# Softmax normalization moved from the output stage to each tile's exit from PSUM, and key tiles reused for value-output weights, in a latent-attention block

## The chip, the cores and the metric

The kernel runs on one core of one Trainium2 chip. A core has four compute engines that run side by side, each with its own instruction queue: TensorE (PE in the profile; its weight loads are listed as PEld), VectorE (DVE), ScalarE (ACT) and GpSimd (POOL). SyncE (SP) only issues transfers. Engines wait for each other through semaphores, and within one queue the instructions run in order: one that waits holds all behind it. POOL's queue, like SP's, can issue DMAs too; such an issue occupies POOL for a time. The metric is the device time of one execution in microseconds (us). The runs shown of the kernel before took 1716.29 us in the median of three (1714.57 to 1717.13).

## The reference

One transformer block on 2048 tokens of width 512, in fp32: attention with low-rank queries and keys/values (16 heads, query rank 384, latent rank 128, head size 128 plus 64 of rotary position), residual and layer norm, then a linear layer with residual and layer norm.

```python
cq   = rms_norm(x @ w_qa.T, q_a_ln_w);  q = (cq @ w_qb.T)        # 16 heads of 128 + 64
ckv  = x @ w_kva.T                                               # 128 + 64
k_pe = rope(ckv[..., 128:]);            ckv_l = rms_norm(ckv[..., :128], kv_a_ln_w)
kv   = ckv_l @ w_kvb.T;                 k_nope, v = split(kv)    # per head
scores = where(causal, -inf, concat(q_nope, rope(q_pe)) @ concat(k_nope, k_pe).T * scale)
attn = softmax(scores)
x = layernorm(x + (attn @ v) @ w_o.T)
x = layernorm(x + x @ (weight * scale[:, None]).T + bias)
```

The softmax's division is what the change is about: every row of `attn @ v` has to be divided by the sum of that row's exponentials at some point.

## The kernel before

**What is kept.** The key half of `w_kvb` is folded into the queries, so that keys are the latent itself. `Kn` (latent, 128 rows) and `Kp` (position) lie in SBUF for all 2048 tokens, each as two fp32r parts whose sum is the fp32 value (`[P, 2, S]`, 16 KB in each partition). `V` is the same latent with tokens on the partitions, as two f16 parts. The value half of `w_kvb` is folded into `w_o`: for each pair of heads a tile `wvo` (`[P, 2, 2, HID]` fp32r, 8 KB in each partition) takes the latent result straight to the output. There are eight pairs of heads.

**Attention.** Queries come in four blocks b = 0 to 3 of 512, each in four tiles qt of 128. For each block, pair p, tile qt and head j, `head_scores` makes the scores by TensorE (L437, mask L440), takes the row maximum on VectorE (L500), and exponentiates on ScalarE (L522), whose accumulator gives the row sums. `head_probs` cuts the probabilities in two f16 parts (ScalarE L553, POOL L554). `turn` transposes them, by VectorE in squares of 32 (L536) and by a DMA on SP's queue through a place in SBUF called `ring`. `values` (L593) multiplies by V on TensorE (L604), in two halves, and lets the result leave PSUM by a ScalarE copy (L609) into a tile `ot`, 128 latent rows by 256 columns (two heads of 128 queries). `put_off` stores `ot` to `ot_d[b][p]` in DRAM: on POOL's queue in block 0 (L321), later on SP's (L329). In block 0 the two heads go together (`pair_scores`, `pair_probs`, L561 to L591), since a tile has at most 512 keys.

**Sums.** `sums_of` gives one small tile for each block and pair, with a column for each tile and head. `settle` runs once a pair is complete: it adds the two halves where a row of scores is cut in two (b > 1, L462), takes the reciprocal of 128 x 8 (L463, L465), transposes it (L467) so that the reciprocals lie along rows, and stores them to `inv_d[b][p]` on SP's queue (L468). All 512 x 2 of a pair go into one such store.

**Output stage.** For each block it takes the pairs in turn. `latent_load` loads the pair's 512 KB of `ot_d` (`o`, L800), and `inv_d` broadcast over the partitions (`iv`, another 512 KB, L806). `latent_split` multiplies the one by the other on POOL (L818) and cuts the product in two fp32r parts, `oh` on ScalarE (L64) and `ol` on VectorE (L65). `accumulate` multiplies by `wvo` on TensorE (L856), 24 matmuls for a pair of a block. Then residual and layer norm (L936 to L952, with POOL at L944), the linear layer (L977) and the second layer norm. The output stage of block 0 and the making of `wvo` (`value_output`, L197, cut at L67 and L68) begin among the last values of block 3.

**Order and memory.** Block 0 is ordered by the scheduler throughout. From block 1 on, TensorE and SP keep the program's order, and VectorE and ScalarE too in the last part of attention; VectorE, ScalarE and POOL otherwise get the order that the scheduler found. Pool `blk` has two buffers for each tag, `ot` among them. The PSUM pool `m`, which values use, has four buffers in block 0 and two later. `wvo0` and `wvo1` lie in the pool `pcr`, `wvo2` and `wvo3` in a pool `pcq` (L895), `wvo4` to `wvo6` in `pc`, which opens where Kn, Kp and V are given up (L918), and `wvo7` in `pcr`.

Of the kernel before, what the change touches and what calls it, by code (L numbers as in the profile page):

```python
# [9 lines left out]
F16 = mybir.dt.float16  # L10
BF16 = mybir.dt.bfloat16
F32 = mybir.dt.float32
F32R = mybir.dt.float32r
# [36 lines left out]
def mla_block(ctx: ExitStack, tc: tile.TileContext, a, out):  # L50
# [22 lines left out]
    wpe_d = [dram.tile([P, 2, LT, 256], F32R, name=f"wpe_d{g}") for g in range(4)]  # L73
    ot_d = [[dram.tile([P, 4, 256], F32, name=f"ot_d{b}_{p}") for p in range(NPAIR)] for b in range(NB)]

    inv_d = [[dram.tile([4, 32, 32], F32, name=f"inv_d{b}_{p}") for p in range(NPAIR)] for b in range(NB)]


    ident = const.tile([P, P], F32, name="ident")
# [21 lines left out]
    ctx_kv = ctx.enter_context(ExitStack())  # L101

    ctx.enter_context(tc.tile_pool(name="pad_l", bufs=1)).tile([P, 8], F32, name="pad_l")
    kv = ctx_kv.enter_context(tc.tile_pool(name="kv", bufs=1))
    Kn = kv.tile([P, 2, S], F32R, name="Kn")
    Kp = kv.tile([P, 2, S], F32R, name="Kp")
    V = [kv.tile([P, 2, 4, P], F16, name=f"V{b}") for b in range(NB)]

# [336 lines left out]
                return mask  # L445
            mask()

    def sums_of(b, p):

        if ("sums", b, p) not in state:  # L450
            state["sums", b, p] = small.tile([P, 2 if b > 1 else 1, 8], F32, tag="sums", name=f"sums{b}_{p}", bufs=2)
            due.append((b, p))
        return state["sums", b, p]

    def settle(now=None):

        while due and due[0] != now:
            b, p = due.pop(0)
            sums = state.pop(("sums", b, p))
            pad = state["pads"][p % 2]  # L460
            if b > 1:
                nc.vector.tensor_tensor(pad[:, :8], sums[:, 0], sums[:, 1], ALU.add)  # L462
                nc.vector.reciprocal(pad[:, :8], pad[:, :8])  # L463
            else:
                nc.vector.reciprocal(pad[:, :8], sums[:, 0])  # L465
            inv = small.tile([P, 32], F32, tag="inv", name=f"inv{b}_{p}", bufs=2)
            nc.vector.transpose(inv, pad)  # L467
            nc.sync.dma_start(inv_d[b][p].rearrange("g t q -> (g t) q"), inv)  # L468

# [3 lines left out]
    def head_scores(pools, b, p, j, qt, nk, prev):  # L473
# [40 lines left out]
        for ti, (v, c0, n, w) in enumerate(tiles):  # L514

            if ti == 0 or b == 3:
                size = nk if b == 2 else n * w
                pr = pools[1].tile([P, size], F32, tag="pr", name=f"pr{b}_{p}_{qt}_{j}_{ti}", bufs=(5, 4, 5)[b - 1])
                parts.append((pr, c0, []))
            x = c0 - parts[-1][1]  # L520
            parts[-1][2].append(slice(x, x + n * w))
            nc.scalar.activation(  # L522
                pr[:, x : x + n * w].rearrange("p (a c) -> p a c", a=n),
                v,
                AF.Exp,
                bias=bias,
                scale=r,
                accum_out=sums_of(b, p)[:, ti, 2 * qt + j : 2 * qt + j + 1],
            )
        return parts  # L530

# [29 lines left out]
    def pair_scores(pool, b, p, qt, nk):  # L561
# [11 lines left out]
        for j in range(2):  # L573
            nc.scalar.activation(  # L574
                pr[:, j, :],
                ps[:, j, :nk],
                AF.Exp,
                bias=bias[:, j : j + 1],
                scale=r,
                accum_out=sums_of(b, p)[:, 0, 2 * qt + j : 2 * qt + j + 1],  # L580
            )
        return pr

# [9 lines left out]
    def values(b, p, qt, nk, PT):  # L593

        kts = nk // P
        v = (PT() if b else PT)[:, : 4 * nk].rearrange("p (q j k r a) -> p j a k q r", j=2, q=4, a=2, k=kts)
        ps = psum["m"].tile([P, 512], F32, tag="m", name=f"o{b}_{p}_{qt}")
        n = 0
        for k in range(kts):
            if k == kts // 2:  # L600
                yield
            vt = V[k // 4]
            for i, l in ((0, 0), (0, 1), (1, 0)):
                nc.tensor.matmul(  # L604
                    ps[:, :256], vt[:, i, k % 4, :], v[:, :, l, k, :], start=n == 0, stop=n == 3 * kts - 1
                )
                n += 1
        ot = blk.tile([P, 256], F32, tag="ot", name=f"ot{b}_{p}_{qt}")
        nc.scalar.activation(ot, ps[:, :256], AF.Copy)  # L609
        put_off(ot_d[b][p][:, qt, :], ot)  # L610
        yield

# [66 lines left out]
    def units(pool, ring, b):  # L679
        lag = min(ring.shape[1] // (2048 * (b + 1)) - 1, 3) if b else 2  # L680

        for p in range(NPAIR):
# [24 lines left out]
            for qt in range(4):  # L707
# [7 lines left out]
                else:  # L715
                    s0, PT = None, place(ring, 2048 * (b + 1), 4 * nk, (b, p) == (2, NPAIR - 1) and qt > 0)
                if nk <= 512:
                    pi = pair_scores(pool, b, p, qt, nk)
                    flush()
                    probs.append(pair_probs(pool, b, p, qt, nk, PT, pi))  # L720
                    if qt == 1:
                        settle((b, p))
                    fill()
                    next(side[0], None)
                    if p and qt % 2:
# [4 lines left out]
                    run_values(lag)  # L730
                else:
                    for j in range(2):
                        if 2 * qt + j == 1:
                            settle((b, p))
                        prepare_output(b, p, 2 * qt + j)
                        prev = probs.pop() if probs else iter(())
                        pi = head_scores(pool, b, p, j, qt, nk, prev)
# [58 lines left out]
    ohl = []  # L796

    def latent_load(b, p, by=nc.sync.dma_start):
        o = state["pcr"].tile([P, 4, 256], F32, tag="o", name=f"o{b}_{p}")
        by(o, ot_d[b][p])  # L800

        n, pool, tag = (4, state["pcr"], "iv") if b == 0 and p < 4 else (1, blk, "qn")
        iv = [pool.tile([P, 4, 8 // n, 32], F32, tag=tag, name=f"iv{b}_{p}_{i}", bufs=2) for i in range(n)]
        for i, v in enumerate(iv):
            src = inv_d[b][p][:, 8 // n * i : 8 // n * (i + 1)].rearrange("g t q -> g (t q)")
            by(v.rearrange("p g t q -> p g (t q)"), src.partition_broadcast(P))  # L806
        state["o", b, p] = o, iv

    def latent_split(b, p):
        if b == NB - 1 and p >= 4:  # L810
            oh, ol = ohl[p - 4]
        else:
            oh = state["pcr"].tile([P, 4, 256], F32R, tag="oh", name=f"oh{b}_{p}")
            ol = state["pcr"].tile([P, 4, 256], F32R, tag="ol", name=f"ol{b}_{p}")
        o, iv = state.pop(("o", b, p))
        parts = o.rearrange("p t q -> p (t q)").rearrange("p (n t g q) -> p n t g q", n=len(iv), g=4, q=32)
        for i, v in enumerate(iv):
            nc.gpsimd.tensor_tensor(parts[:, i], parts[:, i], v.rearrange("p g t q -> p t g q"), ALU.mult)  # L818
        split(o, oh, ol)
        return oh, ol  # L820

    def latent(b, p):
# [58 lines left out]
    with tc.manual_schedule(engines={ET.PE, ET.SP}), ExitStack() as ctx_f:  # L881
# [10 lines left out]

        ps_a = ctx.enter_context(tc.tile_pool(name="ps_a", bufs=4, space=PSUM, reuse_waits="tile"))
        accs = [ps_a.tile([P, HID], F32, tag="acc", name=f"acc0_{t}") for t in range(4)]
        pcq = ctx.enter_context(tc.tile_pool(name="pcq", bufs=1, side="right", reuse_waits="tile"))  # L895
        wvo = state["wvo"]
        wvo += [pcq.tile([P, 2, 2, HID], F32R, name=f"wvo{EARLY + i}") for i in range(2)]
        load_wo(2, blk, "pe")
        latent_load(0, EARLY + 1)
        load_wo(3, blk, "qn")  # L900
# [194 lines left out]
```

## Time and profile before

| | |
|---|---|
| median of the runs shown | 1716.29 us (1714.57 to 1717.13) |
| profiled execution, its own time | 1721.02 us |
| span of the profiled execution | 1719.2 us |
| mean granted TensorE clock | 0.967 |
| attention, query block 0 | about 76 to 265 us |
| block 1; block 2; block 3 | about 265 to 530; 530 to 890; 890 to 1384 us |
| output stage | about 1384 to 1719 us |

The page counts an engine as busy while an instruction of its runs; a DMA-issuing instruction is not counted, though its queue is held by it. Rows of the groups read: line, engine, operation, written tile <- read tiles, shape, count | busy time in all and mean ns of one | idle time just before them and what ended it. A row of a DMA reads: written <- read, issuing engine, count, size of each, median time from issue to landing. For those that the change touches:

```profile
iv<-inv_d SPq DMA_DIRECT2D x28, 512.0 KB, 6.0
```

16 more broadcast loads of `iv` have 128 KB each (block 0, pairs 0 to 3, four for each pair). By shape, the eviction of values at L609 takes 352, 382 and 411 ns (least, median, most), from 76.0 to 1429.9 us.

### The profile page before, as it was taken

What the parts mean: (1) busy time and instruction counts of PE and PEld (TensorE: products, weight loads), DVE (VectorE), ACT (ScalarE), POOL (GpSimd) and SP (SyncE); (2) the same over time, 40 slices, a digit from 0 to 9 for tenths busy, and PEclk for the clock granted to TensorE, in tenths of its full rate; (3) what the DMA queues carried; (4) which work ended last, traced back from release to release, by engine and by line L of the source; (5) the groups of instructions that cost most, each with busy time, mean ns of one, the idle gap of its engine ahead of it and who ended that gap; (6) DMA issues with size and microseconds to landing.
All of it is one profiled execution on the core that took longest, in us unless ns stands there. A gap on an engine that the chain in (4) does not pass through costs nothing. (4 is left out here: it accounts for less than half of the span.)

```text
span 1719.2 us, 27373 instructions
## 1 busy us (share of the span) xinstructions
PE 1597.6 (93%) x9292; PEld 1309.0 (76%) x9292; DVE 1109.0 (65%) x1650; ACT 936.3 (54%) x1593; POOL 836.9 (49%) x606
## 2 busy tenths in 40 slices
PE   8898997999999999999999999999999758888878
PEld 7787876888888888888878888787887536667656
DVE  6567665667677777777766786777677524534364
ACT  5556565566667767677656666566666423111120
POOL 2355663455545655565555556555556432423241
PEclk9899998999999999999999999999999879999989
DMA  7879675667676676666766667557666555445340
GB/s 217 259 211 284 171 213 160 152 184 197 168 222 189 182 178 173 162 174 158 216 169 173 153 156 181 150 133 180 155 165 168 153 158 192 157 123 169 129 137 35
DMA packets 272939, 296.79 MB, mean 173 GB/s; under 512 B 44161, under 2 KB 243201, under 8 KB 271777
## 3 DMA queue, kind: packets, MB, share of 16 engines
q1 hardware_dynamic: 261216, 267.62, 57.8%
q0 software_dynamic: 4672, 17.73, 3.5%
q10 hardware_dynamic: 6912, 9.70, 1.8%
q8 instruction: 74, 1.21, 0.3%
q14 instruction: 65, 0.52, 0.1%
HBM read 99.94 MB, written 35.65 MB: 79 GB/s over the span
## 5 line engine op out<-in xcount | busy, mean ns | idle before, releaser
L554 POOL TENSOR_TENSOR hlpr<-pr,hlpr 128x1024 f16<-128x1024 f32 (+3 forms) x320 | 613.8, 1938 | 499.6 <-ACT hlpr L553 466.0
L437 PE MATMUL s<-Kn,qn 128*128 128x512 f32 (+4 forms) x1920 | 511.8, 374 | 13.8 <-ACT pr L574 8.2
L522 ACT ACTIVATE pr<-s,bias,rq 128x1024 f32<-128x1024 f32 (+3 forms) x320 | 325.3, 1021 | 317.3 <-issue 194.3
L500 DVE TENSOR_REDUCE neg<-s 128x1 f32<-128x1024 f32 (+3 forms) x320 | 311.1, 986 | 157.8 <-PE s L440 90.7
L604 PE MATMUL o<-ring,V 128*128 128x256 f16 x3024 | 376.2, 275 | 9.3 <-DMA ring<-pr 5.5
L437 PEld LDWEIGHTS s<-Kn,qn 128*128 128x128 f32 x1920 | 335.8, 189 | 62.7 <-ACT pr L574 9.3
L536 DVE STREAM_TRANSPOSE pr<-hlpr 128x1024 f32<-128x1024 f32 (+7 forms) x256 | 311.2, 1223 | 97.1 <-POOL hlpr L554 71.8
L437 PE MATMUL s<-Kp,pe 128*128 128x512 f32 (+4 forms) x1280 | 363.6, 364 | 8.2 <-DMA pe<-prod 7.3
L604 PEld LDWEIGHTS <-V 128*128 128x128 f16 x3264 | 302.9, 97 | 86.1 <-issue 34.4
L553 ACT ACTIVATE hlpr<-pr 128x1024 f16<-128x1024 f32 (+3 forms) x320 | 337.8, 1114 | 3.9
L437 PEld LDWEIGHTS s<-Kp,pe 128*128 128x128 f32 x1280 | 234.4, 190 | 39.7 <-DMA pe<-prod 7.5
L818 POOL TENSOR_TENSOR o<-o,iv 128x1024 f32<-128x1024 f32 (+1 forms) x44 | 80.1, 1825 | 191.6 <-DMA o<-ot_d 107.9
L856 PE MATMUL acc<-wvo,oh 128*128 128x512 f32 x448 | 151.1, 419 | 3.4 <-ACT oh L64 2.1
L409 PE MATMUL ps_qn<-cq,wq 128*128 128x512 f32 x576 | 149.4, 405 | 5.0 <-DMA wq<-wq_d 4.7
L409 PEld LDWEIGHTS ps_qn<-cq,wq 128*128 128x128 f32 x576 | 105.8, 192 | 25.4 <-DVE pr L536 3.4
L856 PE MATMUL acc<-wvo,ol 128*128 128x512 f32 x224 | 94.4, 421 | 24.4 <-DVE ol L65 24.4
L856 PEld LDWEIGHTS acc<-wvo,oh 128*128 128x128 f32 x448 | 88.7, 201 | 26.2 <-issue 4.3
L64 ACT ACTIVATE oh<-o 128x1024 fp32r<-128x1024 f32 x28 | 29.6, 1058 | 106.7 <-POOL o L818 88.3
L609 ACT ACTIVATE ot<-o 128x256 f32<-128x256 f32 x128 | 48.5, 379 | 63.5 <-PE o L604 54.0
L68 DVE SCALAR_TENSOR_TENSOR qn<-ps_qn,kvln,qn 128x512 fp32r<-128x512 f32 x64 | 47.5, 743 | 50.3 <-ACT qn L67 50.1
L589 POOL TENSOR_TENSOR hl<-pr,hl 128x128 f16<-128x128 f32 (+3 forms) x64 | 56.8, 907 | 44.4 <-ACT hl L588 44.1
L856 PEld LDWEIGHTS acc<-wvo,ol 128*128 128x128 f32 x224 | 44.9, 200 | 38.6 <-DVE ol L65 28.6
(154 smaller groups left out, 1568.1 us busy)
## 6 DMA issues: line engine op xcount, KB each, us to landing
ring<-pr SPq DMA_DIRECT2D x384, 128.0 KB, 2.7
wq<-wq_d SPq DMA_DIRECT2D x22, 768.0 KB, 5.7
o<-ot_d SPq DMA_DIRECT2D x32, 512.0 KB, 5.9
ring<-pr SPq DMA_DIRECT2D x128, 112.0 KB, 2.6
iv<-inv_d SPq DMA_DIRECT2D x28, 512.0 KB, 6.0
ot_d<-ot SPq DMA_DIRECT2D x97, 128.0 KB, 2.6
ring<-pr SPq DMA_DIRECT2D x128, 96.0 KB, 2.4
ring<-pr SPq DMA_DIRECT2D x64, 192.0 KB, 3.5
```

Source lines behind the costliest of these rows:

```text
L409: nc.tensor.matmul(ps, w[:, i, lt, j * P : (j + 1) * P], cq[:, k, lt, :], start=n == 0, stop=n == 8)
L437: nc.tensor.matmul(ps[:, :w], lhs, K[:, i, c0 : c0 + w], start=n == 0, stop=n == 4 and not by_product)
L500: nc.vector.tensor_reduce(neg[:, ti : ti + 1], v, axis=AX.XY, op=ALU.max, negate=True)
L522: nc.scalar.activation(pr[:, x : x + n * w].rearrange("p (a c) -> p a c", a=n), v, AF.Exp, bias=bias, scale=r, accum_out=sums_of(b, p)[:, ...
L536: nc.vector.transpose(sq.rearrange("p (k c r) -> p k c r", k=4, r=32), words.rearrange("p (c k r) -> p k c r", k=4, r=32))
L553: nc.scalar.activation(hl[:, 0, c], pr[:, c], AF.Copy)
L554: nc.gpsimd.tensor_tensor(hl[:, 1, c], pr[:, c], hl[:, 0, c], ALU.subtract)
L589: nc.gpsimd.tensor_tensor(hl[:, j, 1, :], pr[:, j, :], hl[:, j, 0, :], ALU.subtract)
L604: nc.tensor.matmul(ps[:, :256], vt[:, i, k % 4, :], v[:, :, l, k, :], start=n == 0, stop=n == 3 * kts - 1)
L609: nc.scalar.activation(ot, ps[:, :256], AF.Copy)
L818: nc.gpsimd.tensor_tensor(parts[:, i], parts[:, i], v.rearrange("p g t q -> p t g q"), ALU.mult)
L856: nc.tensor.matmul(acc, l[:, t, c], state["wvo"][p][:, i, j, :], start=p == 0 and j == 0 and n == 0, stop=p == NPAIR - 1 and j == 1 and n ...
```

## The change

Four things are done.

- The sums get one tile for each block, pair and tile of queries (three buffers), and `settle` runs at the start of every tile: a reduction over the two halves where there are two, a reciprocal of 128 x 2, a transpose, and a store of 16 KB into a rotating DRAM tile `rows` (eight buffers). The store is issued from POOL's queue, where it was SP's.
- `values` allocates a tile `iv` of 128 x 256 under the tag `ot`, which has two buffers in all, and loads `rows` into it, broadcast over the partitions: 128 KB in pieces of 256 bytes, from POOL's queue. The result leaves PSUM by a VectorE multiply with `iv`, in place of the ScalarE copy. There are 128 such tiles, so 128 stores, 128 loads and 128 multiplies.
- In the output stage the `iv` loads and the POOL multiplies go; `latent_split` only splits. In all POOL's queue goes from 544 to 746 instructions, SP's from 736 to 667, ScalarE's from 1181 to 1054 and VectorE's from 1597 to 1967.
- V moves into a pool of its own, and the pool of Kn and Kp lives to the end. `wvo2` to `wvo5` are written into the two halves of Kn and of Kp; pool `pcq` is gone, and `pc` holds `wvo6` alone.

```diff
-    inv_d = [[dram.tile([4, 32, 32], F32, name=f"inv_d{b}_{p}") for p in range(NPAIR)] for b in range(NB)]
...
-    kv = ctx_kv.enter_context(tc.tile_pool(name="kv", bufs=1))
+    kv = ctx.enter_context(tc.tile_pool(name="kv", bufs=1))
+    vals_ = ctx_kv.enter_context(tc.tile_pool(name="vals", bufs=1))
...
-    V = [kv.tile([P, 2, 4, P], F16, name=f"V{b}") for b in range(NB)]
+    V = [vals_.tile([P, 2, 4, P], F16, name=f"V{b}") for b in range(NB)]
...
+    def sums_of(b, p, qt):
+
+        key = b, p, qt
+        if ("sums", *key) not in state:
+            state["sums", *key] = small.tile([P, 2, 2 if b > 1 else 1], F32, tag="sums", name=f"sums{b}_{p}_{qt}", bufs=3)
+            due.append(key)
+        return state["sums", *key]
+
+    def settle(now=None, last=None):
+
+        while due and due[0] != now and (last is None or last in due):
+            key = due.pop(0)
+            sums = state.pop(("sums", *key))
+            pad = state["pads"][key[2] % 2]
+            if key[0] > 1:
+                nc.vector.tensor_reduce(pad[:, :2], sums, axis=AX.X, op=ALU.add)
+                nc.vector.reciprocal(pad[:, :2], pad[:, :2])
             else:
-                nc.vector.reciprocal(pad[:, :8], sums[:, 0])
-            inv = small.tile([P, 32], F32, tag="inv", name=f"inv{b}_{p}", bufs=2)
+                nc.vector.reciprocal(pad[:, :2], sums[:, :, 0])
+            name = "_".join(map(str, key))
+            inv = small.tile([P, 32], F32, tag="inv", name=f"inv{name}", bufs=2)
             nc.vector.transpose(inv, pad)
-            nc.sync.dma_start(inv_d[b][p].rearrange("g t q -> (g t) q"), inv)
+            rows = state["rows", *key] = dram.tile([4, 32, 32], F32, tag="rows", name=f"rows{name}", bufs=8)
+            nc.gpsimd.dma_start(rows.rearrange("g t q -> (g t) q"), inv)
...
         ps = psum["m"].tile([P, 512], F32, tag="m", name=f"o{b}_{p}_{qt}")
+        settle(last=(b, p, qt))
+        iv = blk.tile([P, 256], F32, tag="ot", name=f"iv{b}_{p}_{qt}")
+        rows = state.pop(("rows", b, p, qt))[:, :2].rearrange("g t q -> g (t q)")
+        nc.gpsimd.dma_start(iv.rearrange("p (g x) -> p g x", g=4), rows.partition_broadcast(P))
...
         ot = blk.tile([P, 256], F32, tag="ot", name=f"ot{b}_{p}_{qt}")
-        nc.scalar.activation(ot, ps[:, :256], AF.Copy)
+        views = [x.rearrange("p (j g q) -> p j g q", j=2, g=4) for x in (ot, ps[:, :256])]
+        nc.vector.tensor_tensor(*views, iv.rearrange("p (g j q) -> p j g q", g=4, j=2), ALU.mult)
         put_off(ot_d[b][p][:, qt, :], ot)
...
                 if nk <= 512:
+                    settle()
                     pi = pair_scores(pool, b, p, qt, nk)
                     flush()
                     probs.append(pair_probs(pool, b, p, qt, nk, PT, pi))
-                    if qt == 1:
-                        settle((b, p))
...
-                        if 2 * qt + j == 1:
-                            settle((b, p))
+                        if j == 0:
+                            settle()
...
     def latent_load(b, p, by=nc.sync.dma_start):
-        o = state["pcr"].tile([P, 4, 256], F32, tag="o", name=f"o{b}_{p}")
+        o = state["o", b, p] = state["pcr"].tile([P, 4, 256], F32, tag="o", name=f"o{b}_{p}")
         by(o, ot_d[b][p])
-
-        n, pool, tag = (4, state["pcr"], "iv") if b == 0 and p < 4 else (1, blk, "qn")
-        iv = [pool.tile([P, 4, 8 // n, 32], F32, tag=tag, name=f"iv{b}_{p}_{i}", bufs=2) for i in range(n)]
-        for i, v in enumerate(iv):
-            src = inv_d[b][p][:, 8 // n * i : 8 // n * (i + 1)].rearrange("g t q -> g (t q)")
-            by(v.rearrange("p g t q -> p g (t q)"), src.partition_broadcast(P))
-        state["o", b, p] = o, iv
...
-        o, iv = state.pop(("o", b, p))
-        parts = o.rearrange("p t q -> p (t q)").rearrange("p (n t g q) -> p n t g q", n=len(iv), g=4, q=32)
-        for i, v in enumerate(iv):
-            nc.gpsimd.tensor_tensor(parts[:, i], parts[:, i], v.rearrange("p g t q -> p t g q"), ALU.mult)
-        split(o, oh, ol)
+        split(state.pop(("o", b, p)), oh, ol)
...
-        pcq = ctx.enter_context(tc.tile_pool(name="pcq", bufs=1, side="right", reuse_waits="tile"))
         wvo = state["wvo"]
-        wvo += [pcq.tile([P, 2, 2, HID], F32R, name=f"wvo{EARLY + i}") for i in range(2)]
+        wvo += [K[:, i].rearrange("p (a j h) -> p a j h", a=2, j=2) for K in (Kn, Kp) for i in range(2)]
...
-    wvo += [pc.tile([P, 2, 2, HID], F32R, name=f"wvo{p}") for p in range(EARLY + 2, NPAIR - 1)]
+    wvo += [pc.tile([P, 2, 2, HID], F32R, name=f"wvo{p}") for p in range(EARLY + 4, NPAIR - 1)]
```

More of the change, by code (lines that the diff above doesn't have):

```diff
@@ L446, in score @@
             mask()
[L448 to L463, printed above, removed]
-            else:
-                nc.vector.reciprocal(pad[:, :8], sums[:, 0])
-            inv = small.tile([P, 32], F32, tag="inv", name=f"inv{b}_{p}", bufs=2)
+    def sums_of(b, p, qt):
[12 more added lines that the diff above has]
+                nc.vector.reciprocal(pad[:, :2], pad[:, :2])
+            else:
+                nc.vector.reciprocal(pad[:, :2], sums[:, :, 0])
+            name = "_".join(map(str, key))
+            inv = small.tile([P, 32], F32, tag="inv", name=f"inv{name}", bufs=2)
             nc.vector.transpose(inv, pad)
-            nc.sync.dma_start(inv_d[b][p].rearrange("g t q -> (g t) q"), inv)
+            rows = state["rows", *key] = dram.tile([4, 32, 32], F32, tag="rows", name=f"rows{name}", bufs=8)
+            nc.gpsimd.dma_start(rows.rearrange("g t q -> (g t) q"), inv)
     def head_scores(pools, b, p, j, qt, nk, prev):
@@ L527, in head_scores @@
                 scale=r,
-                accum_out=sums_of(b, p)[:, ti, 2 * qt + j : 2 * qt + j + 1],
+                accum_out=sums_of(b, p, qt)[:, j, ti : ti + 1],
             )
@@ L579, in pair_scores @@
                 scale=r,
-                accum_out=sums_of(b, p)[:, 0, 2 * qt + j : 2 * qt + j + 1],
+                accum_out=sums_of(b, p, qt)[:, j, 0:1],
             )
```

## The prediction

> **What bounds the kernel now.** I read the page's totals and its 40 slices first, then busy time by stretch, cut where the stages change, then the waits and the order of time around the gaps. Totals and slices:
>
> ```profile
> PE 1597.6 (93%) x9292; PEld 1309.0 (76%) x9292; DVE 1109.0 (65%) x1650; ACT 936.3 (54%) x1593; POOL 836.9 (49%) x606
> ...
> PE   8898997999999999999999999999999758888878
> ...
> PEclk9899998999999999999999999999999879999989
> ```
>
> TensorE is busy nearly everywhere, with dips near slice 7 (query block 0 ends) and from slice 32 on (attention ends, output stage). By stretch (columns: stretch, length, busy PE, PEld, DVE, ACT, POOL, granted clock, DMA share, GB/s):
>
> ```profile
> 76.00:260.00 184.00, 171.03 (x1158) 148.77 (x1157) 122.87 (x234) 110.96 (x306) 100.25 (x158) 0.99 0.76 221
> ...
> 300.00:530.00 230.00, 229.29 (x1412) 189.68 (x1411) 155.30 (x230) 149.15 (x225) 112.78 (x57) 0.99 0.69 186
> ...
> 1384.00:1404.00 20.00, 0.30 (x2) 0.00 (x0) 3.56 (x6) 0.69 (x1) 6.40 (x6) 0.57 0.66 176
> ...
> 1480.00:1556.00 76.00, 65.04 (x258) 51.16 (x257) 31.66 (x57) 11.93 (x13) 27.53 (x17) 0.89 0.48 139
> ```
>
> Block 1 has TensorE busy 229.29 of 230 us: nothing gained beside it counts there, and anything late enough to stop it costs in full. The idle 20 us at 1384 and the output stage behind it are where time is to be had. The gap, as TensorE, ScalarE and VectorE show it in order of time (start, duration, instruction, idle before it and its releaser):
>
> ```profile
> 1404.20 2.08 PE L197 MATMUL ps_wo<-wo,wv 128*128 128x512 f32 x2 [19.90 <-DVE wvo L68]
> ```
> ```profile
> 1402.67 0.69 ACT L67 ACTIVATE wvo<-ps_wo,kvln_o 128x512 fp32r<-128x512 f32 x1 [18.68 <-DMA inv_d<-inv]
> ```
> ```profile
> 1389.14 0.21 DVE L467 STREAM_TRANSPOSE inv<-pad 128x32 f32<-128x32 f32 x1
> 1403.39 0.75 DVE L68 SCALAR_TENSOR_TENSOR wvo<-ps_wo,kvln_o,wvo 128x512 fp32r<-128x512 f32 x1 [14.04 <-ACT wvo L67]
> ```
>
> One wvo tile can't be written, because its memory (pool pcq) was last held by what a store to inv_d read, and that store stood on SP's queue behind iv loads that waited for POOL. TensorE waits 19.90 us for it. In the waits of the whole kernel the output stage shows as:
>
> ```profile
> POOL o L818 <- DMA o<-ot_d: 107.9, 18, 12.0
> ...
> ACT oh L64 <- POOL o L818: 88.3, 13, 10.4
> ...
> PE acc L856 <- DVE ol L65: 24.4, 8, 5.6
> ```
>
> That is a ring: load o, multiply, split, and the next iv load is held until the multiply is done, with the next o load behind it on SP. Once in order of time: multiply 1528.93 to 1531.3, iv issue 1531.35, out store 1532.44, o issue 1533.57, next multiply 1540.46. All of TensorE's stalls from 1408 to the end add to 39.6 us.
>
> **Part 1: wvo moves into Kn and Kp, inv_d goes.** The wvo write then waits for nothing on SP; Kn and Kp are last read by the final scores, earlier than 1384. Next late is VectorE: its last transpose of the pair ends at 1388.8, so L68 can start near 1390 instead of 1403.39. **−14 us.** The five or six us left of the gap stay.
>
> **Part 2: multiplies and iv loads leave the output stage.** Removed: 44 POOL multiplies and 44 SP loads (40 of L806, 4 of a later put-off). These rows price them, with others used below:
>
> ```profile
> L818 POOL TENSOR_TENSOR o<-o,iv 128x1024 f32<-128x1024 f32 (+1 forms) x44 | 80.1, 1825 | 191.6 <-DMA o<-ot_d 107.9
> ...
> L609 ACT ACTIVATE ot<-o 128x256 f32<-128x256 f32 x128 | 48.5, 379 | 63.5 <-PE o L604 54.0
> ...
> o<-ot_d SPq DMA_DIRECT2D x32, 512.0 KB, 5.9
> ...
> ot_d<-ot SPq DMA_DIRECT2D x97, 128.0 KB, 2.6
> ```
> ```profile
> L65 DVE TENSOR_TENSOR cqst<-ps_cq,cqst 128x256 fp32r<-128x256 f32 x18 | 7.4, 412 | 5.0 <-ACT cqst L64 4.9
> ```
> ```profile
> iv<-inv_d SPq DMA_DIRECT2D x14, 128.0 KB, 5.1
> ```
> ```profile
> L321 POOL DMA_DIRECT2D ot_d<-ot x31 | 18.0, 580 | 27.7 <-ACT ot L609 12.7 <-ACT sq L281 7.7 <-ACT hl L588 4.7
> ```
>
> (The first four are from the page; the fifth from the groups by shape; the sixth from the DMA view of 1300 to 1404; the last from POOL's groups.) A latent (one pair of one block) then needs load 5.9 + split high 1.06 + split low 1.22 = 8.2 us, over two buffers some 4.1 to 4.5; TensorE takes 24 matmuls x 0.228 = 5.5 us for it. So TensorE bounds the stage, and I take 31 of the 39.6 us of stalls as gone: what remains (about 9 us) are layer-norm chains, POOL's lnr and output splits, which have nothing to do with iv. Bounds: 20 (the o load stays late, behind output stores on SP) to 38.
>
> The clock. Full-speed work from 1404 on is about 240 us (747 acc matmuls x 0.228 = 171, 15 linear groups of the FFN x 2.72 = 41, the rest transposes, wvo and last values), against some 300 elapsed; 40 are stalls, so 20 are slow matmuls: a pair of matmuls that takes 0.63 us takes 1.05 for some 3 us after a stall, and the granted clock is 0.89 in the stretch above. The Trainium skill ("TensorE: Matmul & The Clock Gate", What's actually happening) has the cold clock as half of the warm one, given after an idle window. By that rule each stall that goes returns more than itself, by the row only while the rate is seen low. I take two thirds of the 20 us, **13** (0 to 18). Sum of part 2: **−44** (−20 to −56).
>
> **Part 3: normalizing at each tile.** Per tile added: on VectorE a reciprocal 0.16 and transpose 0.20 (rows L463, L467: 194 and 204 ns), in blocks 2 and 3 a sum of about 0.19, and the multiply with one PSUM operand, 0.41 by the cqst row; on POOL's queue a rows store (0.58 by L321) and an iv load. 512 pieces instead of 128: I estimate 0.77 us of issuing, bounds 0.58 to 2.3 (four times L321). Removed: 128 evictions on ScalarE (48.5 us) and 16 sums at L462 (25.2), 32 reciprocals and transposes (12.6), 32 inv_d stores. Net: VectorE +52.5 + 58 − 38 = +73, POOL +128 x 1.35 − 80 = +93 (all of it before 1384), ScalarE −48, SP 76 issues fewer (32 stores, 44 loads). With VectorE 0.67 and POOL 0.54 busy in block 0, the totals fit; the order in which they wait is the matter.
>
> iv and ot share a tag with two buffers, so one iv is alive at a time, and the next iv load waits for this multiply. POOL stands waiting there, with the next tile's probability subtract (L589, L554) behind it, so ScalarE, the turn and TensorE's values are behind too. VectorE stands at the multiply until iv lands, with the row maxima (L500) behind it. Per tile this makes a **chain**: multiply 0.42, in block 0 POOL's store of ot 0.57, iv issue, landing, with handovers. Landing is the disputed price. The Trainium skill ("DMA: Bandwidth & Descriptors", Anatomy of one DMA — SWDGE (gpsimd) path) fits 2.0 us + bytes / 436e3 us: 2.3 us for 128 KB, a chain of 3.4 to 3.5 us, which would cost nothing: sum −58. The row of the same shape (128 KB of 256 B pieces, SP) says 5.1, and POOL's stores land 0.9 us later than SP's of their size (3.5 at L321, 2.6 on the page): 5.0 + 0.9 = 5.9, chain 7.0 (6.3 to 8.5). I take the row, as it has the same pieces.
>
> Another rule speaks against the change: "SBUF — State Buffer" (Who interferes with whom) says POOL's descriptors starve while VectorE runs in its two-port mode; its example is a 620 ns DMA stretched to 3100. By it 256 new POOL DMAs could lose 2.5 us each. The 31 stores at L321 took 542 to 642 ns beside a VectorE 0.67 busy, so I price them by the row.
>
> - Block 0: 31 evictions L609 run from 75.97 to 258.46, 6.08 us apart on average. At 7.0 the chain paces them: the first multiply near 80 (first eviction 75.97, plus most of a landing), so 80 + 30 x 7.0 = 290 for the multiply that stands ahead of block 1's first row maximum on VectorE, which has to run at 266 (first score of block 1 done at 266.4). **+22** (5 to 40).
> - Block 1: a pair takes 28.4 us, 7.1 a tile, the chain 6.5 to 7.2 there (SP stores ot). TensorE has nothing to spare, and the scheduled order sets some multiplies only 2.7 to 4.5 us apart. **+7** (0 to 18).
> - Blocks 2 and 3: 10.5 and 14 us a tile, the iv load is hidden under scores; VectorE rises from about 36 to 39 us of each 50. **+3** (0 to 15).
>
> Sum: −14 − 44 + 22 + 7 + 3 = **−26**: from the profiled execution's 1721.0 (span 1719.2, 1.8 around it) to 1695. The median of the runs shown is 1716.3, 4.7 lower; the same −26 gives **1690**.
>
> **Rivals.**
> - The chain is longer: slower. At 8.5 us a link (iv issue 2.3, or landing 7.5 at block 0's DMA share of 0.76; iv loads of this kind took 7 to 9.5 in busy stretches), block 0 gives 80 + 30 x 8.5 = 335, or +65 with what is behind it, block 1 +30: −58 + 65 + 30 = +37, **1753**. It decides from a link of about 7.65 us, where block 0 costs 43 and block 1 some 12. For: one buffer, and back-to-back pairs of store and load on POOL in the changed order. Against: quiet iv landings of 4.5.
> - iv is hidden after all (link under 6.08): −58 + 3 = −55, **1661**. For: the skill's fit, and slack in block 0, where TensorE is busy 171 of 184. Against: the row.
> - The output stage keeps its stalls, as the 512 KB o load, the longer part of the ring (107.9 against 41.2 us waited for iv), still stands on SP behind output stores: parts 1 and 2 bring −14 − 8, attention +32, so +10, **1726**.
>
> **Chances and range.** Forecast 0.47, its own range 1672 to 1712; long chain 0.27; iv hidden 0.12; stalls kept 0.14. Within 0.2% (3.4 us) no change can be told. Faster: 0.44 of the forecast, the 0.12, 0.01 of the last, 0.57. Same: 0.02 + 0.04 = 0.06. Slower: 0.27 + 0.09 + 0.01 = 0.37. The range takes the third case (1652 and up) and the lower half of the long chain (up to 1748): some 18 in 100 left out.
>
> **What would show it.** The first TensorE gap near 1390 at 6 us, and the output stage's granted clock at 0.95 or above (parts 1, 2); ot multiplies in block 0 about 7.0 us apart with iv as their releaser, and block 1's first scores near 290; iv landing at 5 to 6.5 from POOL; L321-like issues near 0.6. Wrong if iv lands in 3, or takes over 2 us to issue, if TensorE waits in blocks 2 and 3 for values, or if acc still waits for ol by 20 us.

## The result and the profile after

The changed kernel takes 1778.93 us in the median (1777.85 to 1782.98) beside 1716.05 us of the kernel before: a ratio of 1.0371, 95% interval 1.0353 to 1.039. It is slower by 63 us; the prediction had 26 us faster (1690, range 1652 to 1748). Its profiled execution has a span of 1781.1 us and a mean granted clock of 0.959 (0.967 before). Totals and slices from the page:

```profile
PE 1620.3 (91%) x9292; PEld 1322.8 (74%) x9292; DVE 1155.5 (65%) x2018; ACT 899.5 (51%) x1465; POOL 920.7 (52%) x818
...
PE   8888876589888989999999989999999999899998
...
PEclk9899997799998999999999989999999999999999
```

The dip that stood at slice 32 is gone and the last eighth is full. What is new is a hole from slices 5 to 9 and unsteady slices up to 15: the first two query blocks. Two stretches, in the columns of the prediction's table (stretch, length, busy PE, PEld, DVE, ACT, POOL, clock, DMA share, GB/s):

```profile
76.00:260.00 184.00, 156.10 (x999) 133.93 (x999) 120.07 (x254) 84.89 (x236) 105.63 (x170) 0.95 0.80 197
```
```profile
1636.00:1720.00 84.00, 84.00 (x379) 68.79 (x378) 45.62 (x83) 17.30 (x19) 8.94 (x12) 1.00 0.37 121
```

In the first 184 us of block 0 TensorE is busy 156 where it was 171, and it starts 999 matmuls where it started 1158. In the output stage it never stops.

A finer account: the start of the 32nd, 64th, 96th and 128th exit of values from PSUM divides each trace into the four query blocks (the first with the weight preparation) and the output stage. Numbers are us of the profiled spans. The last two columns tell how many buffers iv and ot have, and in what pieces iv is read.

| run | block 0 | block 1 | block 2 | block 3 | output | span | iv, ot buffers | pieces |
|---|---|---|---|---|---|---|---|---|
| before | 275.9 | 273.5 | 373.0 | 507.5 | 289.3 | 1719.2 | no iv in attention | |
| after | 348.5 | 336.0 | 386.9 | 478.0 | 231.6 | 1781.1 | 1, 1 (shared) | 256 B |
| e1 | 309.9 | 297.4 | 371.1 | 479.9 | 233.5 | 1691.8 | 2, 2 | 256 B |
| e2 | 354.8 | 296.8 | 373.5 | 474.8 | 233.2 | 1733.2 | 1, 2 | 256 B |
| e3 | 275.0 | 272.6 | 369.8 | 499.1 | 289.6 | 1706.0 | as before | |
| e4 | 284.4 | 278.0 | 371.6 | 472.8 | 238.5 | 1645.3 | no iv | |
| e5 | 330.4 | 331.5 | 390.3 | 481.3 | 232.4 | 1766.0 | 2, 1 | 256 B |
| e6 | 270.9 | 281.3 | 369.7 | 471.8 | 238.5 | 1632.1 | constant iv | |
| e9 | 322.2 | 298.1 | 375.2 | 476.4 | 234.2 | 1706.1 | 2 (unread), 2 | 256 B |
| e12 | 295.9 | 287.7 | 371.4 | 480.1 | 232.3 | 1667.4 | 2, 2 | 1 KB |
| e13 | 317.5 | 317.0 | 386.6 | 470.0 | 231.8 | 1722.9 | 1, 1 (shared) | 1 KB |

The labels e1 to e13 are the experiments told below; e7, e8, e10 and e11 are given there alone.

After against before: +72.6, +62.5 and +13.9 in blocks 0, 1 and 2; −29.5 and −57.6 in block 3 and the output stage. Both halves of the forecast's sum were too small, the loss by far the more.

The waits of the changed kernel name what stands (engine, waiting instruction, what released it: us in all, times, longest):

```profile
DVE ot L617 <- DMA ot_d<-ot: 90.4, 42, 7.1
...
POOL iv L604 <- DVE ot L617: 79.4, 29, 8.2
...
DVE ot L617 <- DMA iv<-rows: 73.5, 26, 6.9
...
PE o L611 <- DVE ot L617: 36.5, 19, 6.2
```

L617 is the new multiply. It waits for iv, which the prediction spoke of, and longer still for `ot_d<-ot`, which it did not: iv and ot share two buffers, so ot has one as well, and a multiply can't write before the store of the last ot has landed. The end of block 0 shows the iv chain undisturbed, on POOL's queue and then on TensorE (start, duration, instruction, idle before it and its releaser):

```profile
318.30 0.56 POOL L321 DMA_DIRECT2D ot_d<-ot  x1 [5.96 <-DVE ot L617]
318.85 0.76 POOL L604 DMA_DIRECT2D iv<-rows  x1
324.61 0.56 POOL L321 DMA_DIRECT2D ot_d<-ot  x1 [5.00 <-DVE ot L617]
325.16 0.77 POOL L604 DMA_DIRECT2D iv<-rows  x1
```
```profile
337.01 3.86 PE L371 MATMUL ps_pe<-cq,wpe 128*128 128x512 f32 x9 [20.24 <-DVE ot L617]
```

Store, iv issue, five us of landing, multiply, and again; TensorE stands for 20.24 us until the last of these multiplies is done. Block 1 has the other chain, through SP. On VectorE, and on SP's queue before it:

```profile
523.69 0.42 DVE L617 TENSOR_TENSOR ot<-o,iv 128x256 f32<-128x256 f32 x1 [4.72 <-DMA ot_d<-ot]
```
```profile
512.88 5.42 SPq L546 DMA_DIRECT2D ring<-pr  x8
518.34 0.59 SPq L329 DMA_DIRECT2D ot_d<-ot  x1
```

The multiply before this one started at 513.93. Its store had eight ring transfers ahead of it on SP, was issued at 518.34, and landed some five us later; the next multiply waited for that, with row maxima and transposes behind it on VectorE.

In the changed kernel TensorE's waits from 1380 to the end are down to single pieces. The 24.4 us at the `acc` matmuls, which the prediction shows, have become 0.5:

```profile
PE ps_wo L197 <- DVE Kn L68: 5.7, 1, 5.7
...
PE acc L852 <- DVE ohl L65: 0.5, 1, 0.5
```

### The profile page after: what moved, and what is told of

It is laid out like the page before. It is cut to its first block, busy times and chain, and to the rows that moved or that the text cites. A ratio compares the mean times of both kernels' runs of the same rounds, so it can differ in the third digit from the quotient of the medians.

```text
span 1781.1 us, 27777 instructions
## 1 busy us (share of the span) xinstructions
PE 1620.3 (91%) x9292; PEld 1322.8 (74%) x9292; DVE 1155.5 (65%) x2018; ACT 899.5 (51%) x1465; POOL 920.7 (52%) x818
## 4 chain that ended last, share of the span: by engine, by line
PE 47%; DMA 12%; SPq 6%; DVE 6%; issue 5%; ACT 3%; POOL 2%; DVEq 0%; ACTq 0%; POOLq 0%
PE s L437 18%; PE o L611 11%; PE acc L852 9%; SPq L546 4%; DMA ot_d<-ot 4%; PE ps_qn L409 3%; DMA ring<-pr 3%; DVE pr L539 2%; POOL hlpr L557 2%; PE ff L972 2%; DMA iv<-rows 2%; DMA wq<-wq_d 2%; ACT pr L525 1%; PE ps_pe L371 1%; SPq L329 1%
## 5 line engine op out<-in xcount | busy, mean ns | idle before, releaser
L437 PE MATMUL s<-Kn,qn 128*128 128x512 f32 (+4 forms) x1920 | 518.9, 378 | 15.9 <-ACT pr L577 8.5
L409 PE MATMUL ps_qn<-cq,wq 128*128 128x512 f32 x576 | 159.1, 424 | 28.1 <-DVE ot L617 25.3
L604 POOL DMA_DIRECT2D iv<-rows x128 | 98.4, 769 | 135.4 <-DVE ot L617 79.4
L617 DVE TENSOR_TENSOR ot<-o,iv 128x256 f32<-128x256 f32 x128 | 53.1, 415 | 177.2 <-DMA ot_d<-ot 90.4
L939 POOL TENSOR_TENSOR lnr<-lnt,nhalf 128x1 f32<-128x1 f32 x32 | 21.2, 670 | 204.5 <-DVE lnt L938 204.5
L471 POOL DMA_DIRECT2D rows<-inv x128 | 72.7, 568 | 86.9 <-DVE inv L469 78.2
L371 PE MATMUL ps_pe<-cq,wpe 128*128 128x512 f32 x288 | 77.6, 417 | 27.9 <-DVE ot L617 20.9
L371 PEld LDWEIGHTS ps_pe<-cq,wpe 128*128 128x128 f32 x288 | 55.0, 200 | 40.0 <-DVE ot L617 21.3
L67 ACT ACTIVATE qn<-ps_qn,kvln 128x512 fp32r<-128x512 f32 x64 | 43.8, 684 | 66.3 <-PE ps_qn L409 65.9
L852 PE MATMUL acc<-wvo,oh 128*128 128x512 f32 x224 | 72.6, 406 | 0.0
```

Of the source, the lines that this page charges most:

```text
L371: nc.tensor.matmul(ps, w[:, i, lt, x * P : (x + 1) * P], cq[:, k, lt, :], start=n == 0, stop=n == 8)
L409: nc.tensor.matmul(ps, w[:, i, lt, j * P : (j + 1) * P], cq[:, k, lt, :], start=n == 0, stop=n == 8)
L437: nc.tensor.matmul(ps[:, :w], lhs, K[:, i, c0 : c0 + w], start=n == 0, stop=n == 4 and not by_product)
L471: nc.gpsimd.dma_start(rows.rearrange("g t q -> (g t) q"), inv)
L604: nc.gpsimd.dma_start(iv.rearrange("p (g x) -> p g x", g=4), rows.partition_broadcast(P))
L852: nc.tensor.matmul(acc, l[:, t, c], state["wvo"][p][:, i, j, :], start=p == 0 and j == 0 and n == 0, stop=p == NPAIR - 1 and j == 1 and n ...
```

## The experiments

Two theories stood at the start. **S, slots**: the single buffers make VectorE and POOL stand. **Q, queues**: 256 issues on POOL and 128 multiplies on VectorE cost it, whatever the buffers. The first four runs part them and measure the gains alone. The scheduler orders POOL, VectorE and ScalarE anew in each kernel, so that a few us in one block mean little: e4 and e6, neither of which loads iv, differ by 13 in block 0. In e1, e2 and e5 to e12 a staging tag of the weight preparation has three buffers for four, to make room; it touches block 0 only. No run took that alone. e6, which has it too, has the shortest block 0 of all runs (270.9), so it can cost little there.

**e1: a tag of its own for iv.**

```diff
-        iv = blk.tile([P, 256], F32, tag="ot", name=f"iv{b}_{p}_{qt}")
+        iv = blk.tile([P, 256], F32, tag="iv", name=f"iv{b}_{p}_{qt}", bufs=2)
```

> The changed kernel with a tag of its own for iv (two buffers), so that ot has its two buffers back; to make room, a staging tag of the weight preparation has three buffers for four. Theory S (one iv slot and one ot slot make VectorE and POOL stand still): multiplies no longer wait for DMA ot_d<-ot (90.4 us in the changed kernel) nor much for iv<-rows (73.5), block 0's last evictions come near 270 to 285 in place of 348, block 1 takes some 275 in place of 336 us; time 1635 to 1665 us. Theory Q (the 256 issues on POOL's queue and the multiplies on VectorE cost it, whatever the slots): block 0 and block 1 stay within 20 us of the changed kernel's, time 1745 to 1780.

1698.48 us, ratio to before 0.9902 (0.988 to 0.9924), between the two forecasts. S holds in direction: two more buffers of 1 KB in each partition turn a loss of 63 us into a gain of 16. It does not hold in size: blocks 0 and 1 stay 34 and 24 us above before.

**e2: only ot's buffer is given back** (as e1 with `bufs=1`).

> As e1, but one buffer for iv and two for ot: only the ot slot is given back. Theory S with the ot slot as what costs block 1, and the iv slot as what costs block 0: block 1 falls from 336 to below 285 us, block 0's 31st eviction stays near 300 to 336, time 1690 to 1720. If the iv slot costs both blocks: block 1 stays above 320 and time is 1750 to 1780. Theory Q: 1750 to 1780 too, but then e1 is as slow.

1734.26 us, ratio 1.0106 (1.0084 to 1.0128), 14 us above what S had expected of it. Block 1 falls from 336.0 to 296.8, as far as in e1, block 0 doesn't fall at all. What is left is the wait for iv:

```profile
DVE ot L617 <- DMA iv<-rows: 60.4, 18, 6.4
```

**e3: keys hold wvo, nothing else changes.**

```diff
-    kv = ctx_kv.enter_context(tc.tile_pool(name="kv", bufs=1))
+    kv = ctx.enter_context(tc.tile_pool(name="kv", bufs=1))
+    vals_ = ctx_kv.enter_context(tc.tile_pool(name="vals", bufs=1))
...
-        wvo += [pcq.tile([P, 2, 2, HID], F32R, name=f"wvo{EARLY + i}") for i in range(2)]
+        wvo += [K[:, i].rearrange("p (a j h) -> p a j h", a=2, j=2) for K in (Kn, Kp) for i in range(2)]
```

> The kernel before with only the second part of the change: Kn and Kp live on and hold wvo2 to wvo5; sums, iv loads and the POOL multiplies stay as they were. Prediction's part 1: the gap of 19.90 us before wvo shrinks by 14 us, the rest of the output stage stays: 1700 to 1704. Rival: the wait moves on to the next thing on SP (o or iv loads of the output stage), and time is within 5 us of before, 1711 to 1717.

1707.17 us, ratio 0.9954 (0.994 to 0.9969), 3 us above the forecast: 5 to 10 us faster by the times, 13.2 by the profiled spans. In the trace the stop of 19.90 us before wvo is 5.74:

```profile
1383.76 2.08 PE L198 MATMUL ps_wo<-wo,wv 128*128 128x512 f32 x2 [5.74 <-DVE Kn L68]
```

**e4: no division.** The iv loads are left out and results leave PSUM by the copy.

> The changed kernel without the division: sums, reciprocals and the stores of rows stay, the iv loads are left out, and results leave PSUM by the ScalarE copy of before. It shows what the output stage gives when attention pays only for settle and the rows stores. From the changed kernel's own stages (block 3 and output 87 us shorter than before): 1625 to 1645. If the output stage gave only what the prediction took (58): 1655 to 1665. Theory Q's part that lies in settle and the rows stores would show as block 0 ending after 290 us and time above 1680.

1650.4 us, ratio 0.9625 (0.9606 to 0.9644), between the two forecasts. The output stage and block 3 together take 711.3 us where before took 796.8: −85, and e3 has 8 of it. Blocks 0 and 1 are 8.5 and 4.5 us longer than before with settle and the stores of rows in them.

**e5: the other half of e2**, two buffers for iv and one for ot.

> The other half of e2: two buffers for iv, one for ot. From e1 and e2 (block 1 of 336 us in the changed kernel, 297 in both e1 and e2; block 0's 45 us only with the second iv buffer): theory 'ot slot in block 1, iv slot in block 0' expects block 0 ended near 310 (its 32nd eviction), block 1 near 336 us with waits of VectorE for ot_d<-ot of 70 us or more, time 1735 to 1755. If either slot alone is enough to tie block 1, block 1 is under 310 us and time near 1700.

1769.17 us, ratio 1.028 (1.0243 to 1.0316), above the range expected. Block 1 is at 331.5 and block 2 at 390.3, with

```profile
DVE ot L617 <- DMA ot_d<-ot: 138.4, 61, 9.4
```

So block 1 (and 2) is ot's buffer. Block 0 needs both: either alone gives −18 or +6, both together −39.

**e6: the multiply alone**, e4 with a constant tile of ones for iv.

```diff
+    same = const.tile([P, 256], F32, name="same")
+    nc.vector.memset(same, 1.0)
...
-        nc.gpsimd.dma_start(iv.rearrange("p (g x) -> p g x", g=4), rows.partition_broadcast(P))
+        iv = same
```

(The edit is against the changed kernel, whose multiply stays.)

> e4 with the multiply instead of the copy: results leave PSUM on VectorE, multiplied by a constant tile of ones, with no iv load. Leaves out the division. e1 is 48 us above e4, nearly all in blocks 0 and 1 (25 and 19). Theory 'the multiply's place in VectorE's queue costs it': time 1680 to 1700, as e1. Theory 'the iv loads do (POOL's queue held, landings)': 1650 to 1660, as e4.

1640.85 us, ratio 0.9528 (0.9492 to 0.9563), below both forecasts: not slower than e4, in block 0 even 13 us shorter. No cost of the multiply on VectorE shows. The 60 us between the spans of e6 and e1 come with the iv loads: their issues, their time on the DMA engines and the wait for them.

**e7: iv loads of blocks 1 and 2 issued a tile earlier**, into four buffers.

> e1 with iv loads of blocks 1 and 2 issued one tile after their rows are stored, into four buffers of a pool of its own, instead of when values begin. If block 1's remaining 19 us over e4 are waits for iv slots and landings: block 1 280 to 288 us in place of 297, time 1680 to 1690. If they are POOL's and VectorE's queues: unchanged, 1693 to 1702.

1696.27 us, 0.9872 (0.9827 to 0.9917); block 1 293.9. Neither more buffers nor an earlier issue gives what is missing; by the expectation that leaves the queues of POOL and VectorE.

**e8: block 0 divided in the output stage as before.**

> e1, but block 0 keeps the sums for each pair, the copy out of PSUM and the multiply in the output stage (8 of 32 latents); blocks 1 to 3 are divided tile by tile. Block 0 back to 276 to 280 us (310 in e1); the output stage keeps its stalls for 8 latents of 32, with the 20 us wait for wvo gone: 10 to 20 us of e1's gain lost. Time 1675 to 1690, which would beat both kernels. If block 1's start inherits what block 0's end paid: 1690 to 1700.

1707.9 us, 0.993 (0.9909 to 0.9951). Block 0 is back at 280.3, but block 3 takes 519.0 in place of 479.9: its last pair again has iv loads of the output stage in the way (TensorE waited 9.5 us at one of them, VectorE's multiply up to 17.7 for an iv). What one end gains, the other loses and more: the run is 9 us slower than e1, which neither forecast had.

**e9: iv loaded by POOL as in e1, but read by nobody.**

> e4 with the iv loads of e1 on POOL's queue (two buffers), which nobody reads: results leave PSUM by the ScalarE copy, undivided. Leaves out the division. Block 0 takes 310 us in e1, 284 in e4 and 271 in e6. Theory 'POOL's queue': the 256 issues and POOL's waits in order hold up its probability subtracts; block 0 is above 300 us, time above 1675. Theory 'the wait of VectorE for the landed iv' (multiply behind iv): block 0 near 280 to 288 us and time near 1650.

1711.5 us, 0.9982 (0.9966 to 0.9998). Block 0 at 322.2 is even above e1, although no instruction reads iv; e4, the same kernel without the loads (and with the staging tag whole), has 284.4. So the loads cost more than the wait for them. In TensorE's waits from 80 to 310 us the turned probabilities come later than in e4, whose line stands first, then e9's:

```profile
PE o L607 <- DMA PT<-pr: 17.5, 4, 11.2
```
```profile
PE o L611 <- DMA PT<-pr: 29.3, 7, 9.6
```

PT is moved by SP, not by POOL. These waits are 12 us of the 38. This is what the expectation had given to POOL's queue, but a load that stands in the way of others on the DMA engines would show the same.

**e10 and e11: iv loads issued by SP**, in all blocks and in block 0 only.

```diff
-        nc.gpsimd.dma_start(iv.rearrange("p (g x) -> p g x", g=4), rows.partition_broadcast(P))
+        nc.sync.dma_start(iv.rearrange("p (g x) -> p g x", g=4), rows.partition_broadcast(P))
```

> e1 with the iv loads issued by SP instead of POOL (rows still by POOL). Theory 'POOL's queue': block 0 falls to 285 or less in place of 310 and block 1 to 285 in place of 297, time 1655 to 1670. Rival: SP's ring transfers are held by iv loads that wait for a buffer: blocks 1 to 3 grow, time above 1700.

1881.39 us, 1.0982 (1.0946 to 1.1019): SP keeps the program's order from block 1 on and reaches an iv load where its values begin; VectorE waits 202 us for iv, and blocks 1 and 2 grow to 357.2 and 435.4.

> As e10, but SP issues the iv loads of block 0 only, where the scheduler orders SP too; POOL issues the others. Theory 'POOL's queue': block 0 at 285 or less, block 1 at 297 as in e1, time 1668 to 1680. If block 0 stays above 300, landing and VectorE's order are what costs.

1712.44 us, 0.9988 (0.9974 to 1.0002), block 0 331.5. With no iv load on POOL's queue block 0 is 22 us longer than in e1, so it isn't this queue alone that costs. The run doesn't clear POOL either, for SP, which moves PT, now has the loads and stands for them, most of all for their rows (80 to 310 us):

```profile
SPq L604 <- DMA rows<-inv: 14.2, 3, 6.1
```

Theory Q in its pure form fell with e1, where the same issues and multiplies cost 80 us less; how much of the rest is a queue's stays open.

What e1, e9 and e11 share is the transfer itself. The DMA view of block 1 from 320 to 520 us shows it, first for e6, then for e1 (q0 is POOL's queue, q1 holds SP's: packets, MB, share of the 16 engines' time; then issues with count, size and median us to landing):

```profile
q1 hardware_dynamic: 38308, 35.68, 67.2%
q0 software_dynamic: 800, 0.41, 0.9%
...
ring<-pr SPq DMA_DIRECT2D x48, 96.0 KB, 2.4
```
```profile
q0 software_dynamic: 1952, 3.56, 21.9%
...
ring<-pr SPq DMA_DIRECT2D x52, 96.0 KB, 3.9
...
iv<-rows POOLq DMA_DIRECT2D x24, 128.0 KB, 5.4
```

24 loads of 128 KB took 21.0% (21.9 less the 0.9 of e6) of 16 engines for 200 us: 28 us of one engine for each. In e6 q1 moved 35.68 MB in 67.2%, which is 7.9 us for 128 KB. So an iv load from POOL's queue holds the DMA engines 3.6 times as long as a ring transfer of its size. The ring transfers, for which the values wait, land later beside it: the median of those of 96 and 80 KB went from 2.4 and 2.3 us to 3.9 and 3.8.

The loads of e11 set a limit to this. Block 0 from 80 to 260 us, for e4, e9 and e11:

```profile
PT<-pr SPq DMA_DIRECT2D x28, 64.0 KB, 3.0
```
```profile
q0 software_dynamic: 4593, 13.25, 39.9%
q1 hardware_dynamic: 22518, 19.47, 34.7%
...
PT<-pr SPq DMA_DIRECT2D x22, 64.0 KB, 6.0
```
```profile
q1 hardware_dynamic: 34674, 22.44, 42.3%
q0 software_dynamic: 3456, 10.21, 17.4%
...
PT<-pr SPq DMA_DIRECT2D x20, 64.0 KB, 5.2
```

From e9 to e11 24 iv loads move from q0 to q1. q0 loses 22.5 points and q1 gains 7.6: of 16 engines for 180 us that is 27 us of one engine for each load issued by POOL, and about 9 for the same load, in the same pieces, issued by SP. PT still lands late and block 0 is no shorter. So in these runs the long hold belongs to small pieces from POOL's queue, not to small pieces as such, and the hold alone does not explain the late landings.

**e12: the same load in pieces of 1 KB.** Reciprocals are stored so that a tile's 256 lie together; buffers as in e1.

```diff
-            rows = ... dram.tile([4, 32, 32], F32, tag="rows", ...)
-            nc.gpsimd.dma_start(rows.rearrange("g t q -> (g t) q"), inv)
+            rows = ... dram.tile([32, 4, 32], F32, tag="rows", ...)
+            nc.gpsimd.dma_start(rows.rearrange("t g q -> g t q"), inv)
...
-        nc.gpsimd.dma_start(iv.rearrange("p (g x) -> p g x", g=4), rows.partition_broadcast(P))
+        nc.gpsimd.dma_start(iv, rows.partition_broadcast(P))
```

> e1 with the rows laid out so that what iv reads is one piece of 1 KB for each partition instead of four of 256 bytes; as many loads, bytes, stores and instructions on every engine, on the same queue. In e1's trace 24 iv loads of block 1 (3.1 MB) take 21.0% of the 16 DMA engines for 200 us, where 36 MB of ring transfers take 68%; ring and PT transfers land later in every run that has the iv loads, whoever issues them and whether the multiply waits or not (e1, e9, e11). Theory 'the DMA engines' time, by number of pieces': share of the software queue in block 1 falls from 21.9% to 10% or less, iv lands in 4 us or less in place of 5.5, block 0 takes 275 to 290 us in place of 310, block 1 280 to 287 in place of 297, time 1640 to 1665. Rival 'reading the same DRAM rows by 128 partitions, or POOL's order, is what costs': within 8 us of e1, 1690 to 1705.

1670.04 us, ratio 0.9743 (0.9719 to 0.9768), the best of all and faster than both kernels. In the same window:

```profile
q0 software_dynamic: 1937, 3.59, 9.3%
...
iv<-rows POOLq DMA_DIRECT2D x24, 128.0 KB, 3.9
```

The bytes are the same and the share is less than half. The ring transfers of 96 and 80 KB land in 2.5 and 2.9 us, where e1 had 3.9 and 3.8. Block 1 is 9.7 us shorter than in e1 and block 0 14, somewhat less than expected, and the time is 5 us above its forecast. An issue on POOL became shorter too, 555 ns in place of 764 (median), so POOL's time has a part in this gain that the run doesn't separate from the DMA engines'.

**e13: the changed kernel, buffers untouched, with e12's pieces.**

> The changed kernel itself (one slot for iv, one for ot) with the 1 KB pieces of e12. If slots and pieces are separate costs that add: block 0 near 320 (348 in the changed kernel), block 1 near 320 (336), time 1725 to 1745. If the slots only cost because iv lands late (chain of 6.5 us in the changed kernel with landing 5.5): the chain falls to 4.5 us, below the 6.08 us in which block 0 makes a tile, and block 0 comes near 285; block 1 keeps its waits for ot_d<-ot, near 325; time 1675 to 1715.

1727.1 us, 1.0076 (1.005 to 1.0101). The last multiplies of block 0 are 4.6 to 5.6 us apart in place of 6.2 to 7.3, yet block 0 ends at 317.5 and block 1 takes 317.0. That is the first expectation, of two separate costs, in blocks and time; only, they don't simply add: in spans, pieces alone give −58, buffers alone −89, both −114.

## Why the prediction was wrong

**Part 1** (wvo into the keys, −14) was right: the gap went from 19.90 to 5.74 us in e3, VectorE's pair is late next as said, and the span fell by 13.2. The times show 5 to 10.

**Part 2** (−44, bounds 20 to 56) had the mechanism, and both its terms were too small: from e3 to e4 block 3 and the output stage together lose 77 us. From block 3's first exit to the end, for e3 and then e4 (stretch, length, busy PE, PEld, DVE, ACT, POOL, clock, DMA share, GB/s):

```profile
917.34:1706.00 788.66, 718.60 (x3832) 571.67 (x3830) 472.17 (x644) 349.14 (x474) 359.58 (x198) 0.96 0.57 153
```
```profile
934.00:1645.40 711.40, 692.05 (x3832) 560.37 (x3830) 455.60 (x710) 349.47 (x474) 299.09 (x184) 0.99 0.55 146
```

TensorE stands for 19 us in place of 70, and the same matmuls keep it busy 27 us less at a clock of 0.99 in place of 0.96. The step had 31 us of stops and 13 of slow matmuls. It left 9 us of the 39.6 standing, of which hardly any stayed; it left out two stops of 5.2 and 3.6 us before 1404, in block 3's end, which went too; and it took two thirds of 20 us for the clock. The rival in which the o load keeps the stalls is refuted: the o loads landed in 3.6 us in place of 5.9.

**Part 3 failed**: +32 in all, measured +149 (72.6, 62.5 and 13.9). Its prices were good: an iv issue 0.77 us, as estimated (the estimate shows no working beyond its bounds, so the exact hit is in part luck); landing 5.5, estimated 5.9; a multiply 0.415; a pure link, the last of block 0, 6.57 on average from 303.66 to 336.53, estimated 7.0. The row was the right choice over the 2.3 us of the Trainium skill's fit ("DMA: Bandwidth & Descriptors", Anatomy of one DMA — SWDGE (gpsimd) path), and no issue was stretched as the rule on starved descriptors would have it ("SBUF — State Buffer", Who interferes with whom): 256 issues had means of 568 and 769 ns, the longest 647 and 801, and iv landed no sooner from SP (5.6 us, e10). The page ties that rule to certain operations of VectorE; whether one of these ran beside an issue stays open. The page's example of 620 ns made 3100 stands in its section "A bandwidth-pool intuition that's wrong (but worth ruling out)". Two slips are small: 290 and 335 against 266 are 24 and 69, where the text went on with 22 and 65; and block 1's 28.4 us a pair holds for the pairs with no other work among them, the rest take 33 to 36.

Three steps failed in place of the prices:

- *"one iv is alive at a time"* counted half of the shared tag. ot has one buffer too, and a multiply waits for the store of the ot before it. In block 1 the text even took "SP stores ot" as shortening the chain; the store stands on SP behind ring transfers, and lengthens it. Giving ot its buffer back (e2) takes 39 us from block 1 and 13 from block 2; leaving it with one while iv has two (e5) leaves block 1 at 331.5. This is the greater part of block 1's +62.
- *"At 7.0 the chain paces them: [...] 80 + 30 x 7.0 = 290"* took the chain as running without a break from the first tile. The multiplies of block 0 come 8.66 us apart on average (76.77 to 336.53), with single gaps of 10 to 15: whoever waits for the multiply (TensorE for PSUM, POOL's stores, settle) makes the next tile late, and a link then starts late. Two buffers on both sides take 39 us away.
- *"Landing is the disputed price"*: a load of 512 pieces was priced by its issue and by when it lands, and what it keeps others from was put at nothing. With enough buffers and nobody waiting for it (e9) it still costs block 0 38 us and block 1 20 against e4; with larger pieces (e12) block 0 gets 14 back and block 1 10. That this cost is there is shown; whether it is the time on the DMA engines or the queue that issues it is not, as e11 and e12 change both.

The rival of a longer chain came nearest in time (1753) and named the wrong reason: its link of 8.5 us, by a longer issue or landing, wasn't there. The threshold of 7.65 us for a link was therefore no guide: the kernel lost with links of 6.6.

**Open**: e12's span is still 35 us above e6's, 25 of it in block 0. In block 1 the landings suggest the DMA engines: with larger pieces the ring transfers land almost as early as without iv loads. In block 0 e11 speaks against the engines' time as the whole cause. No run divided it from the order on POOL's and SP's queues; nor was it tried to have reciprocals on all partitions without a DMA.

## What to carry to other kernels

When a new tile joins a pool's tag, count for every tile of that tag how many buffers are left and what frees each, a store's queue and landing among it: the chain that costs may be that of the tile that was there first. A small broadcast load is to be priced twice, by its landing and by what it delays in others, on the DMA engines and on the queue that issues it; longer pieces of the same bytes helped in both kernels where they were tried. A chain's link times the count is a lower bound of its length: here every other wait started a link late (8.66 us apart, with pure links of 6.57).

## What the runs showed of the hardware

A 128 KB broadcast load from DRAM in 512 pieces of 256 bytes, issued by POOL, took 28 us of one DMA engine's time, 3.6 times a 128 KB ring transfer; issued by SP it took about 9 (e11 against e9), and yet landed no sooner over the whole kernel (5.6 us in e10, 5.5 in e1). In 128 pieces of 1 KB, by POOL, it took (9.3 − 0.9)% of the same window, about 11 us. In that window it landed in 5.4 us and 3.9, and its issue on POOL took 764 and 555 ns. Not expected either: moving 128 exits from PSUM from ScalarE to VectorE, the busier engine of the two (65% and 51% in the changed kernel), showed no cost (e6 against e4).
